# A projection as seven products of halves: the third pass of a two-layer attention block

## The chip, the cores and the metric

The kernel runs on one core of a Trainium2 chip. Everything is float32. The metric is the device time of one launch in microseconds (us), taken as the median of several executions. The profile and the trace come from one further execution. In them PE is TensorE (PEld its weight loads), DVE is VectorE, ACT is ScalarE, POOL is GpSimd and SP is SyncE, whose queue issues the DMA transfers.

## The reference

The input is `x` of shape (8, 256, 64, 64): eight images of 256 channels. Two layers are computed one after the other.

```python
# layer 0: softmax attention over keys from a 4x4-strided convolution
xr  = layernorm_c(conv(x, w_sr, stride=4))
q   = w_q @ x;  k, v = split(w_kv @ xr)
x   = x + gamma_s * (w_out @ softmax(q k / sqrt(32)) v)
# layer 1: relu linear attention on two sets of q, k, v
qkv = w_qkv @ x
agg = grouped_1x1(depthwise_5x5(qkv))
for part in (qkv, agg):                      # 32 heads of 8 channels each
    q, k, v = relu(part.q), relu(part.k), part.v with a column of ones
    o   = q @ (k.T @ v);  att = o[:, :8] / (o[:, 8] + 1e-15)
p   = w_proj @ concat(att_qkv, att_agg)      # 256 x 512 times 512 x pixels
y   = x + batchnorm(p)                       # a scale inv and a shift per channel
```

The change is in the last two lines. `w_proj` has 256 rows and 512 columns. Its input, for every pixel, is 256 channels of attention on `qkv` (called `att` in the kernel's third pass) and 256 channels of attention on `agg` (called `agg` there).

## The kernel before, in words

**Three passes.** The first pass computes layer 0 and the `qkv` planes, and writes both to device memory. The second pass computes the convolution, the sums k.T v of both parts, and the whole attention of the `agg` part. It writes the latter to the scratch tensors `attd`, one of shape (256, 2, 4, 512) for each image. The second pass works in 64 units of 32 channels of one image. In `applied(u, par)` it turns a tile `tok` of (pixel, channel) to (channel, pixel) with one DVE transpose, once for each of two column parities `par`. `stored(u, par)` writes each parity to memory in a transfer of its own, of 256 KB.

**The third pass** computes the attention of the `qkv` part, the projection, the scale and shift, and the sum with `x`. It works in 64 steps: 8 images, 2 halves of the image, and 4 pixel classes `cls` (the row and column parity of a pixel inside a 2x2 cell, as the planes were written). A step covers 512 pixels, in four groups of 128 that are named `f`, and all 256 output channels. In a step:

- `loads(n)` issues the transfers: `raw` (the q planes), `xs` (the x values), and every fourth step `agg`, 2 MB for half an image. When the fourth class of a half is done, the result tile `y` of 2 MB is stored.
- `flat(n)` makes `q` from `raw` with a ReLU, in four ACT instructions, one for each 128 channels and column parity.
- `applied(n, i)` for i = 0, 1 multiplies `q` with the block-diagonal sums `kvm` (four matmuls of 144 columns into `n`). ACT adds an epsilon to the denominators (`den`), DVE takes their reciprocals and multiplies them in, which gives `tok`.
- `turned(n, i)` transposes `tok` on PE into `at` (four 128x128 transposes), and ACT copies it to `att`.
- `proj(n, oc)` for the two output halves `oc` accumulates four matmuls of 512 columns in one PSUM bank `p` (two from `att`, two from `agg`). Two ACT instructions apply scale and shift and put the two column parities in their places in `z`. Two DVE instructions add `xs` into `y`.

A float32 matmul runs on PE as two passes, each with a weight load of its own, so the counts of the profile are two for each matmul; a transpose is one pass.

**What sets the order.** The kernel is written in program order, and a scheduler orders each engine's instructions from it by priorities and expected durations. The order is then fixed: each engine works through its own list, and waits on semaphores where an operand or a buffer is not ready. Tiles come from pools with a fixed number of buffers, and a new tile waits until all readers of the old one in its place are done. In the third pass `turned` runs half a step behind `applied`, and `proj` one step behind. The PSUM pools `p`, `n` and `at` each hold two tiles; a tile of `p` is one bank.

Of the kernel before, what the change touches and what calls it, by code (L numbers as in the profile page):

```python
# [27 lines left out]
F32 = mybir.dt.float32  # L28
# [4 lines left out]
P = 128  # L33
C = 256
# [926 lines left out]
def second_pass(ctx: ExitStack, tc: tile.TileContext, a, planes, kd, vd, wtd, kvd, attd):  # L961
# [234 lines left out]
    def applied(u, par):  # L1196
        t, k, b = units[u]
        q, bd = qs[u], bds[u]
        pn = bank("ng", f"ng_{u}_{par}", 1, 1024).rearrange("p (h n) -> p h n", h=4)
        for h in range(4):  # L1200
            nc.tensor.matmul(pn[:, h, : P + 16], q[:, par, h], bd[:, h], start=True, stop=True)
        den = late.tile([P, 2, 4, 16], F32, tag="den", name=f"den_{u}_{par}")
        nc.scalar.activation(den[:, 0], pn[:, :, P : P + 16], AF.Identity, bias=eps)
        nc.vector.reciprocal(den[:, 1], den[:, 0])
        tok = late.tile([P, 16, D0], F32, tag="tok", name=f"tok_{u}_{par}")
        nc.vector.tensor_tensor(
            tok.rearrange("p f (h e) -> p h f e", e=D1),
            pn[:, :, :P].rearrange("p h (f e) -> p h f e", e=D1),
            den[:, 1].unsqueeze(3).to_broadcast([P, 4, 16, D1]),
            ALU.mult,  # L1210
        )
        att = two.tile([P, 512], F32, tag="att", name=f"att_{u}_{par}", bufs=4)
        nc.vector.transpose(att, tok.rearrange("p f e -> p (f e)"))
        done[u, par] = att


    def stored(u, par):
        t, k, b = units[u]
        c0 = P * t + D0 * k
        tc.keep_in_program_order(  # L1220
            nc.sync.dma_start(attd[b][c0 : c0 + D0, par].rearrange("c j n -> j c n"), done.pop((u, par)))
        )

    positive(0)
    paired(0, 1)
    for u in range(n_all + 3):
        p, q, r = u - 1, u - 2, u - 3
        now, was, conv, out = u < n_all, 0 <= p < n_all, 0 <= q < n_all, 0 <= r < n_all
        if 0 < u < n_all:
            summed_raw(u)  # L1230
        if u + 1 < n_all:
            load_tokens(u + 1)
        if 0 < p < n_all:
            load_cells(p, 0)
        if was:
            stored_raw(p)
        if r > 0:
            stored(r - 1, 0)
            stored(r - 1, 1)
        if was:  # L1240
            summed(p)
        if now:
            convolve(u, 1, 2)
        if out:
            applied(r, 0)
        if u + 1 < n_all:
            paired(u + 1, 1)
        if now:
            convolve(u, 1, 0)
            if u == 0:  # L1250
                summed_raw(u)
            ended_raw(u)
            convolve(u, 1, 1)
        if u + 2 < n_all:
            load_cells(u + 2, 1)
        if was:
            ended(p)
        if conv:
            paired(q, 0)
            convolve(q, 0, 2)  # L1260
        if out:
            applied(r, 1)
        if conv:
            convolve(q, 0, 0)

        if u + 1 < n_all:
            positive(u + 1)
        if was:
            spread(p)
        if conv:  # L1270
            convolve(q, 0, 1)
        if now and u + B < n_all:
            b = units[u][2]
            load_weights(u + B - b, 1 if b < 4 else 0, b % 4)
    stored(n_all - 1, 0)
    stored(n_all - 1, 1)

# [1 line left out]
def third_pass(ctx: ExitStack, tc: tile.TileContext, a, planes, x2d, kvd, attd, out):  # L1281
# [10 lines left out]
        for tag in ("p", "n", "at")  # L1292
    }


    steps = [(b, half, cls) for b in range(B) for half in range(2) for cls in range(4)]
    n_all = len(steps)
    kvms, aggs, raws, xss, flats, atts, ys = {}, {}, {}, {}, {}, {}, {}

    msk = data.tile([P, P], F32, tag="msk", name="msk", bufs=1)  # L1300
    nc.sync.dma_start(msk, a.mask)
# [21 lines left out]
    def loads(n):  # L1323
# [10 lines left out]
                ],  # L1334
            )
        raws[n] = raw
        xs = data.tile([P, 2, 4, P], F32, tag="xs", name=f"xs_{n}", bufs=4)
        for c in range(2):
            nc.sync.dma_start(
                xs[:, c],  # L1340
# [5 lines left out]
        if cls == 0:  # L1346

            g = data.tile([P, 2, 2, 1024], F32, tag="agg", name=f"agg_{n}")
            for t in range(2):
                nc.sync.dma_start(  # L1350
                    g[:, t], attd[b][t * P : (t + 1) * P, :, 2 * half : 2 * half + 2].rearrange("c q j n -> c q (j n)")
                )
            aggs[b, half] = g.rearrange("p t q (j f n) -> p t (q j) f n", j=2, f=16)


    def flat(n):
        b, half, cls = steps[n]
        q = flattened.tile([P, 2, 4, P], F32, tag="q", name=f"q_{n}")
        col = cls % 2
        src = raws.pop(n).rearrange("p t f (y x) -> p t f y x", x=NB + 1)  # L1360
        for t in range(2):
            for par in range(2):
                nc.scalar.activation(
                    q[:, t, :, par * 64 : par * 64 + 64].rearrange("p f (y x) -> p f y x", y=8),
                    src[:, t, :, :, col + par : col + par + NB - 1 : 2],
                    AF.Relu,
                )
        flats[n] = q

    loads(0)  # L1370
# [18 lines left out]
    nc.vector.tensor_sub(shift, vec[:, 3], shift)  # L1389


    def applied(n, i):
        b, half, cls = steps[n]
        q, kvm = flats[n], kvms[b]
# [13 lines left out]
        )  # L1408
        return tok

    def turned(n, i, tok):
        if i == 0:
            atts[n] = late.tile([P, 2, 4, P], F32, tag="att", name=f"att_{n}")
        pa = psums["at"].tile([P, 512], F32, tag="at", name=f"at_{n}_{i}").rearrange("p (j n) -> p j n", j=4)
        for j in range(4):
            nc.tensor.transpose(pa[:, j], tok[:, j], ident)
        nc.scalar.copy(  # L1417
            atts[n][:, :, 2 * i : 2 * i + 2].rearrange("p t f n -> p f t n"),
            pa.rearrange("p (f t) n -> p f t n", f=2),
        )  # L1420

    def proj(n, oc):
        b, half, cls = steps[n]
        if cls == 0 and oc == 0:
            ys[b, half] = results.tile([P, 2, HW // 2], F32, tag="y", name=f"y_{b}_{half}")
        y = ys[b, half]
        yv = y.rearrange("p c (y a i x b j) -> p c a b i j y x", y=8, a=2, i=2, x=NB, b=2, j=2)
        ps = psums["p"].tile([P, 512], F32, tag="p", name=f"p_{n}_{oc}")
        for j in range(4):
            if j < 2:  # L1430
                src = atts[n][:, j].rearrange("p f (q n) -> p f q n", q=4)
            else:
                src = aggs[b, half][:, j - 2, :, 4 * cls : 4 * cls + 4].rearrange("p q f n -> p f q n")
            nc.tensor.matmul(  # L1434
                ps.rearrange("p (f q n) -> p f q n", f=4, q=4),
                wproj[:, j, oc * P : (oc + 1) * P],
                src,
                start=(j == 0),
                stop=(j == 3),
            )  # L1440
        z = late.tile([P, 4, P], F32, tag="z", name=f"z_{n}_{oc}")
        for par in range(2):
            nc.scalar.activation(  # L1443
                z.rearrange("p f (y x) -> p f y x", x=NB)[:, :, :, par::2],
                ps.rearrange("p (f q y x) -> p f q y x", f=4, q=2, y=8)[:, :, par],
                AF.Identity,
                bias=shift[:, oc : oc + 1],
                scale=inv[:, oc : oc + 1],
            )
        xs = xss[n]  # L1450
        for i in range(2):
            nc.vector.tensor_add(  # L1452
                yv[:, oc, cls // 2, cls % 2, i],
                z[:, 2 * i : 2 * i + 2].rearrange("p f (y x) -> p f y x", x=NB),
                xs[:, oc, 2 * i : 2 * i + 2].rearrange("p f (y x) -> p f y x", x=NB),
            )
        if cls == 3:
            cols = slice(half * (HW // 2), (half + 1) * (HW // 2))
            ready.append((out[b].rearrange("(c p) n -> p c n", p=P)[:, oc, cols], y[:, oc]))

    flat(0)
    last, ready = None, []
    for n in range(n_all + 1):
        if n + 2 < n_all:
            loads(n + 2)

            for dst, src in ready:
                tc.keep_in_program_order(nc.sync.dma_start(dst, src))
            ready = []
        if n + 1 < n_all:  # L1470
            flat(n + 1)
        for i in range(2):
            tok = applied(n, i) if n < n_all else None
            if last is not None:
                turned(*last)
            last = (n, i, tok) if n < n_all else None
            if n > 0:
                proj(n - 1, i)
        if n > 0:
            xss.pop(n - 1), atts.pop(n - 1)  # L1480
    for dst, src in ready:
        nc.sync.dma_start(dst, src)

# [2 lines left out]
def kernel_body(ctx: ExitStack, tc: tile.TileContext, a, out):  # L1486
# [15 lines left out]
    vd = [scratch(f"v_{b}", [8, NB2 + 2, NB2 + 2, P]) for b in range(B)]  # L1502
    kvd = {(b, t): scratch(f"kv_{b}_{t}", [4, 4, D0, D0 + 1]) for b in range(B) for t in range(2)}

    attd = [scratch(f"att_{b}", [C, 2, 4, 16 * D0]) for b in range(B)]
    wtd = [scratch(f"wt_{j}", [P, 16, 6 * P]) for j in range(4)]

    first_pass(tc, a, fine, planes, x2d, kd, vd, wtd)
# [120 lines left out]
```

## Time and profile before

The median is 4034.7 us (three runs, 4033.01 to 4037.88). The profiled execution spans 4031.7 us, at a granted TensorE clock of 0.99.

| stage | from, to (us) | PE busy | DVE busy | ACT busy | POOL busy |
|---|---|---|---|---|---|
| end of the second pass | 3220 to 3358 | 100% | 63% | 28% | 39% |
| passage to the third | 3358 to 3396 | 72% | 37% | 35% | 0% |
| third pass, steady | 3396 to 4009 | 99% | 45% | 49% | 0% |
| its end | 4009 to 4031.7 | 52% | 24% | 23% | 0% |

The figures are the busy times of the stages in a view by stretches, divided by their lengths. In the steady stage PE works nearly without a gap, DVE and ACT for half of the time, and POOL not at all. The DMA engines are busy for 0.71 of it.

### The profile page before, as it was taken

Reading aid. Unit: us, or ns where it says so; the run is one execution under the profiler, and the core shown is the slowest. Engines: PE = TensorE matmul, PEld = TensorE weight load, DVE = VectorE, ACT = ScalarE, POOL = GpSimd, SP = SyncE. Lnnn points to the kernel's source line nnn. Section 1 sums busy time; section 2 is a strip of 40 time slices with the busy share of each in tenths; the row PEclk is TensorE's granted clock in tenths of the full one; section 3 lists DMA queues with packets and bytes.
Section 4 is the critical chain, followed back from the end, with each engine's and each line's share of the span. In section 5 each row is a group of like instructions: output and inputs, shape, how many; then the busy total and the mean of one; then the engine's idle time right before and its main releaser. Section 6 shows DMA issues by size and latency. Waiting matters only on the chain. (4 is left out here: it accounts for less than half of the span.)

```text
span 4031.7 us, 69469 instructions
## 1 busy us (share of the span) xinstructions
PE 3967.1 (98%) x27266; PEld 2322.3 (58%) x27266; DVE 1943.0 (48%) x2724; ACT 1666.0 (41%) x3505; POOL 1207.0 (30%) x1234
## 2 busy tenths in 40 slices
PE   8999999999999999999999999999999998999998
PEld 4433433434334344343337888888888886565565
DVE  2554344343443434434444566666666664444443
ACT  2345455454554544545552222222222223454454
POOL 2333233332333333323333344444444440000000
PEclk9999999999999999999999999999999999999999
DMA  7655435344444344443539888778778756767674
GB/s 236 205 178 155 128 92 146 103 105 144 104 136 115 95 143 105 132 115 92 145 102 253 240 227 236 219 220 237 218 220 237 202 168 172 234 197 235 199 231 138
DMA packets 588321, 691.32 MB, mean 171 GB/s; under 512 B 62160, under 2 KB 431312, under 8 KB 583760
## 3 DMA queue, kind: packets, MB, share of 16 engines
q1 hardware_dynamic: 587984, 686.79, 59.7%
q8 instruction: 216, 3.54, 0.4%
q14 instruction: 121, 0.99, 0.1%
HBM read 412.54 MB, written 274.10 MB: 170 GB/s over the span
## 5 line engine op out<-in xcount | busy, mean ns | idle before, releaser
L786 POOL TENSOR_TENSOR e<-e,e 128x512 f32<-128x512 f32 x512 | 651.9, 1307 | 1204.1 <-PE av L775 1190.2
L799 DVE RECIPROCAL rden<-den 128x512 f32<-128x512 f32 x128 | 429.7, 3357 | 688.0 <-PE den L791 688.0
L764 ACT ACTIVATE e<-sc 128x512 f32<-128x512 f32 x1024 | 529.3, 602 | 419.2 <-PE sc L758 419.2
L834 PE MATMUL qkv<-x,wqkv 128*128 128x512 f32 x1536 | 701.1, 599 | 0.0
L834 PEld LDWEIGHTS qkv<-x,wqkv 128*128 128x128 f32 x1536 | 285.3, 190 | 372.7 <-issue 354.0
L1085 PE MATMUL cv<-w,c 128*128 128x128 f32 x3072 | 386.9, 280 | 4.9 <-POOL c L1029 4.9
L1085 PEld LDWEIGHTS cv<-w,c 128*128 128x128 f32 x3072 | 360.9, 193 | 33.5 <-issue 27.0
L853 DVE STREAM_TRANSPOSE turned<-qkv 128x512 f32<-128x512 f32 x256 | 177.3, 707 | 338.8 <-ACT stage L843 282.0
L758 PE MATMUL sc<-q,kk 32*128 32x512 f32 x2048 | 324.2, 640 | 11.0 <-DVE x L810 7.3
L1127 PE MATMUL sums<-vq,r 128*32 128x288 f32 x4096 | 303.1, 410 | 0.0
L1452 DVE TENSOR_TENSOR y<-z,xs 128x256 f32<-128x256 f32 x256 | 142.6, 644 | 315.9 <-ACT z L1443 290.9
L1101 ACT ACTIVATE r<-s 128x512 f32<-128x512 f32 x256 | 160.5, 627 | 299.9 <-DVE s L1100 299.5
L843 ACT COPY stage<-qkv 128x512 f32<-128x512 f32 x256 | 150.1, 586 | 304.3 <-PE qkv L834 294.6
L775 PE MATMUL av<-e,vv 128*32 128x512 f32 x2048 | 274.3, 608 | 0.0
L1443 ACT ACTIVATE z<-p,bn 128x256 f32<-128x256 f32 x256 | 133.7, 578 | 314.5 <-PE p L1434 240.6
L1089 PE MATMUL cv<-c,w 128*128 128x128 f32 x2048 | 256.4, 279 | 0.0
L743 PE MATMUL q<-x,wq 128*128 128x512 f32 x512 | 253.8, 618 | 0.0
L1434 PE MATMUL p<-att,wproj 128*128 128x512 f32 x512 | 249.4, 609 | 2.2 <-ACT att L1417 2.2
L1092 ACT COPY both<-cv 128x512 f32<-128x512 f32 x128 | 75.0, 586 | 421.8 <-PE cv L1085 364.8
L1434 PE MATMUL p<-agg,wproj 128*128 128x512 f32 x512 | 242.3, 596 | 0.0
L1089 PEld LDWEIGHTS cv<-c,w 128*128 128x128 f32 x2048 | 242.2, 194 | 0.0
L671 PE MATMUL sr<-x,wsr 128*128 128x256 f32 x1024 | 234.6, 385 | 7.1 <-DMA wsr<-in_w_sr_dram 7.1
(121 smaller groups left out, 5107.8 us busy)
## 6 DMA issues: line engine op xcount, KB each, us to landing
vq<-v SPq DMA_DIRECT2D x256, 384.0 KB
planes<-stage SPq DMA_DIRECT2D x256, 289.0 KB
d<-planes SPq DMA_DIRECT2D x128, 578.0 KB
raw<-planes SPq DMA_DIRECT2D x128, 272.0 KB
x<-in_xp_dram SPq DMA_DIRECT2D x64, 512.0 KB
wsr<-in_w_sr_dram SPq DMA_DIRECT2D x128, 256.0 KB
x<-x SPq DMA_DIRECT2D x128, 256.0 KB
k<-turned SPq DMA_DIRECT2D x256, 128.0 KB
```

Source lines behind the costliest of these rows:

```text
L671: nc.tensor.matmul(ps[:, oc], w[:, ci, oc * P : (oc + 1) * P], xt[:, ci, f * NK : (f + 1) * NK], start=(f == ci == oc == 0), stop=(f == R ...
L743: nc.tensor.matmul(ps, consts["wq"][:, ci, c * P : (c + 1) * P], x_tiles[b][:, ci, s * QB : (s + 1) * QB], start=(ci == 0), stop=(ci == 1),)
L758: nc.tensor.matmul(scs[h], kks[b][rows, c, kc * P : (kc + 1) * P], qs[rows], start=True, stop=True)
L764: nc.scalar.activation(e, scs[h], AF.Exp, scale=D0**-0.5)
L775: nc.tensor.matmul(sums["av"][cols], vvs[b][:, kc, c * P + h * D0 : c * P + (h + 1) * D0], es[h], start=(kc == 0), stop=(kc == 1),)
L786: nc.gpsimd.tensor_tensor(es0[h], es0[h], es1[h], ALU.add)
L799: nc.vector.reciprocal(r, den)
L834: nc.tensor.matmul(ps, consts["wqkv"][:, ci, j * P : (j + 1) * P], x_tiles[b][:, ci, s * QB : (s + 1) * QB], start=(ci == 0), stop=(ci == 1),)
L1085: nc.tensor.matmul(out, x, m, start=(da == 0), stop=(da == 1))
L1089: nc.tensor.matmul(out, m, x, start=(da == 0), stop=(da == 1))
L1127: nc.tensor.matmul(ps[h * D0 : (h + 1) * D0, : 36 * D1].rearrange("p (r n e) -> p r n e", r=3, e=D1), kt[:, par, h, 2 * r + c], vq[:, r : ...
L1434: nc.tensor.matmul(ps.rearrange("p (f q n) -> p f q n", f=4, q=4), wproj[:, j, oc * P : (oc + 1) * P], src, start=(j == 0), stop=(j == 3),)
```

## The change

The projection of a step is a product of a 256 x 512 matrix and a 512 x 512 matrix of pixels. It is cut into a 2 x 2 scheme: the rows of `w_proj` into two output halves `oc`, its columns into the `agg` and the `att` half, and the pixels into two halves i = 0, 1. Done directly these are eight products of quarters. The change uses the scheme of Strassen, in Winograd's form, which needs seven. Each product is a 128 x 256 by 256 x 256 product: two matmuls of 256 columns, four passes. The weights of the seven are the quarters `a11`, `a12`, `a21`, `a22` and their combinations `s1` to `s4` and `minus`, formed once at the start of the pass, with the scale `inv` multiplied in. The right sides are `agg` and `att` of either half and four combinations `t1` to `t4`, formed in every step: `t1` on DVE (`early_side`), the other three on POOL (`late_sides`).

The four quarters of the result share partial sums. The change keeps three regions in PSUM: `x` and `y` side by side in one bank, `z` in another. Four products go to `x` one after the other, and each adds to what is there. After each, ACT or DVE reads the sum so far before the next product comes on top of it.

Around this, three things follow. The `agg` output of the second pass is stored with the column parities interleaved, in one transfer of 512 KB for each unit, so that `flat` needs two ACT instructions instead of four, and the results need no reordering by parity. The loop of the third pass is one step longer, since the products run two steps behind `applied`. Half of the additions of `xs` move from DVE to POOL.

```diff
-        att = two.tile([P, 512], F32, tag="att", name=f"att_{u}_{par}", bufs=4)
-        nc.vector.transpose(att, tok.rearrange("p f e -> p (f e)"))
+        if par == 0:
+            done[u] = two.tile([P, 16, D0, 2], F32, tag="att", name=f"att_{u}")
+        nc.vector.transpose(done[u][:, :, :, par], tok)
...
         for t in range(2):
-            for par in range(2):
-                nc.scalar.activation(... 128x256 ..., AF.Relu)
+            nc.scalar.activation(
+                q[:, t].rearrange("p f (y x) -> p f y x", y=8), src[:, t, :, :, col : col + NB], AF.Relu
+            )
...
+    nc.vector.tensor_mul(wproj, wproj, wide.unsqueeze(1).to_broadcast([P, 4, C]))
+    a11, a12, a21, a22 = (wproj[:, k : k + 2, oc * P : (oc + 1) * P] for oc in range(2) for k in (2, 0))
+    nc.vector.tensor_add(s1, a21, a22)
+    nc.vector.tensor_sub(s2, s1, a11)
+    nc.vector.tensor_sub(s3, a11, a21)
+    nc.vector.tensor_sub(s4, a12, s2)
+    nc.scalar.mul(minus, a22, -1.0)
...
+    def early_side(n):
+        nc.vector.tensor_sub(sides[n][:, 0], agg(n, 1), agg(n, 0))
+    def late_sides(n):
+        nc.gpsimd.tensor_tensor(t2, raw1, t1, ALU.subtract)
+        nc.gpsimd.tensor_tensor(t3, raw1, agg(n, 1), ALU.subtract)
+        nc.gpsimd.tensor_tensor(t4, t2, raw0, ALU.subtract)
...
+    def first_products(n):
+        xy, zb = (psums["p"].tile([P, 512], F32, tag=f"p{i}", name=f"p{i}_{n}", bufs=1) for i in range(2))
+        product(n, x, a11, agg(n, 0), first=True)
+        nc.scalar.activation(parts[n][:, 0], x, AF.Identity, bias=shift[:, 0:1])
+        product(n, y, a12, atts[n][:, 0].rearrange("p t (j n) -> p t j n", j=2))
+        nc.vector.tensor_add(quarter(n, 0, 0), split(parts[n][:, 0]), split(y))
+    def second_products(n):
+        product(n, x, s2, sides[n][:, 1])
+        nc.scalar.activation(parts[n][:, 1], x, AF.Identity, bias=shift[:, 0:1])
+        product(n, z, s1, sides[n][:, 0], first=True)
+        nc.scalar.activation(parts[n][:, 2], z, AF.Identity, bias=shift[:, 1:2])
+    def third_products(n):
+        product(n, x, s3, sides[n][:, 2])
+        nc.vector.tensor_add(quarter(n, 1, 1), split(parts[n][:, 2]), split(x))
+    def fourth_products(n):
+        product(n, x, minus, sides[n][:, 3])
+        nc.scalar.activation(quarter(n, 1, 0), split(x), AF.Identity, bias=shift[:, 1:2])
+        product(n, z, s4, atts.pop(n)[:, 1].rearrange("p t (j n) -> p t j n", j=2))
+        nc.vector.tensor_add(quarter(n, 0, 1), split(parts.pop(n)[:, 1]), split(z))
...
+        (nc.vector if i else nc.gpsimd).tensor_tensor(
+            yv[:, oc, cls // 2, cls % 2, i], outs[n][:, oc, i]..., xss[n][:, oc, 2 * i : 2 * i + 2]..., ALU.add,
+        )
...
-    for n in range(n_all + 1):
+    for n in range(n_all + 2):
+        m = n - 2
+        first_products(m); flat(n + 1); applied(n, 0); early_side(n)
+        finished(m, 0, 0); second_products(m); turned(n - 1, 1); late_sides(n - 1)
+        third_products(m); applied(n, 1); turned(n, 0)
+        finished(m, 1, 1); fourth_products(m); finished(m, 1, 0); finished(m, 0, 1)
```

The loop at the end is given as the order of its calls; the conditions for the first and last steps are left out.

## The prediction

> **What bounds the kernel now.** I first read the busy shares over the span, where PE has 98%, and then the third pass alone, since the change works only there and in two small places before it. The groups of instructions from 3400 to 4000 us show what a step of it is made of: columns are the count, the busy time, the mean ns of one, and the idle time before it with its releaser.
>
> ```profile
> L1434 PE MATMUL p<-att,wproj 128*128 128x512 f32 x481 | 232.5, 606 | 0.0
> ...
> L1398 PE MATMUL n<-kvm,q 128*128 128x144 f32 x962 | 147.6, 286 | 0.0
> ...
> L1452 DVE TENSOR_TENSOR y<-z,xs 128x256 f32<-128x256 f32 x240 | 133.8, 645 | 292.5 <-ACT z L1443 267.5 <-DMA agg<-att 10.5 <-DMA xs<-x 7.0
> ...
> L1363 ACT ACTIVATE q<-raw 128x256 f32<-128x256 f32 x240 | 89.6, 465 | 0.0
> ...
> L1417 ACT COPY att<-at 128x512 f32<-128x512 f32 x120 | 70.8, 590 | 8.0 <-PE at L1416 3.8
> ```
>
> Its PE groups have no idle time; ACT and DVE wait for each other and for PE. So PE's list sets the time. A PE duration contains the drain of the pipeline; the pace is read from starts. The timeline of PE in one step (start, duration, what, passes):
>
> ```profile
> 3612.47 0.41 PE L1398 MATMUL n<-kvm,q 128*128 128x144 f32 x2
> 3612.71 0.60 PE L1416 MATMUL at<-ident,tok 128*128 128x128 f32 x4
> 3613.15 1.88 PE L1434 MATMUL p<-att,wproj 128*128 128x512 f32 x4
> 3614.87 1.88 PE L1434 MATMUL p<-agg,wproj 128*128 128x512 f32 x4
> 3616.58 1.14 PE L1398 MATMUL n<-kvm,q 128*128 128x144 f32 x8
> 3617.56 0.60 PE L1416 MATMUL at<-ident,tok 128*128 128x128 f32 x4
> 3618.00 0.90 PE L1398 MATMUL n<-kvm,q 128*128 128x144 f32 x6
> 3618.84 1.98 PE L1434 MATMUL p<-att,wproj 128*128 128x512 f32 x4
> 3620.66 1.88 PE L1434 MATMUL p<-agg,wproj 128*128 128x512 f32 x4
> 3622.38 0.41 PE L1398 MATMUL n<-kvm,q 128*128 128x144 f32 x2
> ```
>
> A step is 3622.38 - 3612.47 = 9.91 us. Starts give 0.4285 us for a pass of 512 columns (1.715 for four), 0.1225 for 144 columns (0.98 for eight), 0.11 for a transpose. Sixteen, sixteen and eight of them are 6.86 + 1.96 + 0.88 = 9.70. The other 0.21 lies at 3618.84, the one product that has to wait (for ACT's copy of `att`): six passes that need 0.735 take 0.84, and the four behind them take 1.82 instead of 1.715. So a wait that PE meets costs the wait itself plus about 0.11 for a weight load that is no longer hidden.
>
> **What the Trainium skill says.** "TensorE: Matmul & The Clock Gate", section "Architectural detail: the array is 16x 32x32, not 1x 128x128", says that PE's queue can pull weight loads ahead of running matmuls. The trace agrees: passes of 144 columns follow each other every 0.12 us although a load lasts 0.19. "PSUM — Partial Sum Buffer", section "PSUM bank collisions raise a hardware error", says that two engines must not be in one bank at the same time, even at other columns, and that semaphores should guard whole banks. In the changed kernel's list PE indeed waits for DVE's read of `y` before it writes `x` in the same bank. No such pair is in the third pass before. "SBUF — State Buffer", section "Who interferes with whom", says that a DVE instruction with two SBUF inputs and a GpSimd instruction that reads SBUF exclude each other for the whole instruction. The second pass shows it:
>
> ```profile
> 2663.49 1.28 POOL L1061 TENSOR_TENSOR red_raw<-kq 128x512 f32<-128x512 f32 x1 [1.19 <-ACT kq L1068]
> 2663.86 1.49 DVE L1025 TENSOR_TENSOR c<-d 128x544 f32<-128x544 f32 x1 [0.65 <-DMA d<-planes]
> ...
> 2664.85 1.09 POOL L1062 TENSOR_TENSOR red_raw<-red_raw 128x256 f32<-128x256 f32 x1
> 2665.28 1.25 DVE L1026 TENSOR_TENSOR c<-d 128x544 f32<-128x544 f32 x1
> ```
>
> The DVE operation takes 0.72 elsewhere; here it ends 0.58 after POOL's end, and POOL's next ends 0.59 after DVE's.
>
> **PE's work after.** Seven products of four passes are 28 passes of 256 columns. The first pass has such a shape: sixteen of `sr` take from 680.65 to 684.10, so 0.2155 each, loads hidden. That is 6.03 us instead of 6.86. The other passes stay: 6.03 + 1.96 + 0.88 = 8.87.
>
> **The waits that come with it.** PE's order in a step of the changed kernel is: `n0` (2 passes), x1 (`agg` by `a11`), `n0` (6), y, z, three transposes, x2 (`s2`), one transpose, `n1` (4), x3 (`s3`), `n1` (4), four transposes, x4 (`minus`), z again (`s4`). Every x waits for a reader of the bank. From the trace: PE's last issue to ACT's start 0.25 (3612.47 to 3612.72), ACT's end to PE 0.05. ACT reading 256 columns: a copy takes 0.37 (L726), and a bias pointer adds 0.1 (64 columns with bias 0.31, 36 without 0.19), so 0.47. DVE on 256 columns from PSUM: 0.42 (L687). Laid out from 0:
>
> - x1 ends at 1.11. ACT has read it, and y may start, at 1.11 + 0.25 + 0.47 + 0.05 = 1.88; `n0` fills until 1.84. Wait 0.04, load 0.11.
> - y ends at 2.85, z at 3.71, transposes at 4.04. DVE gets to y only behind the reciprocal (0.53) and `tok` (0.69) of `n0`: 2.45 to 3.77; then 0.42 less 0.10 overlap, at PE by 4.14. Wait 0.10, load 0.11: x2 ends at 5.11.
> - x3 needs ACT's read of x2: 5.88, against 5.71 filled. Wait 0.17, load 0.11: ends at 6.85.
> - x4 needs DVE's read of x3 at 7.57; `n1` and transposes fill until 7.78. No wait. It ends at 8.64, z at 9.50.
> - The next x1 needs ACT's read of x4. In ACT's list this stands behind `den` of `n1`, two `flat` and an `att` copy, started at 7.34 + 0.25 and spaced 0.19, 0.50, 0.47, 0.50 (an operation's 0.115 overlap with the next as in the trace; a `flat` of 512 elements as L1101, 0.62). It ends at 9.72, so PE may go at 9.77, against 9.75.
>
> This gives 9.50 without the last wait and 9.63 with it and its load. If the weight load is hidden even behind a wait, the same walk gives 9.33. I take 9.50.
>
> **ACT, DVE, POOL.** ACT sheds two `flat`, and has four reads of 0.47 for four `z` of 0.58. DVE sheds two y additions, and gets `t1` (0.69 as L800, 512 elements from SBUF twice) and three reads: 2x0.53 + 2x0.69 + 3x0.42 + 2x0.64 + 0.69 = 5.7 us in a step. POOL gets three of 512 elements (1.27, the unhindered L1061) and two y additions of 256 (0.73 as L1062; with strided output up to 0.9, no row): 5.3 to 5.6. `t2` to `t4` have nearly a step until PE needs them. Three DVE operations (two y, `t1`) can each be held for up to 1.13 by POOL; in my layout two are, y behind `t2` and the last y behind `t4`, and DVE still reaches the next reciprocal in time.
>
> **Edits at nothing.** The second pass's transposes write every other element: at most tens of ns each in a DVE that idles 37% there, behind a PE at 100%. The larger `att` and `agg` transfers move the same bytes; DMA is at 0.71 and would go to 0.74. The weight combinations (some 3.5 us of DVE) fall in the passage, where PE waits for `raw` until 3388.
>
> **Ends.** Before, from the last `n` (4009.2) PE needs 12.9 us, the last y 2.4, the store 7.2: 22.5. After, a rest of 2.2 and two steps of products without fill remain (6.0 and its waits each): about 17.8 for PE, 1.3 for y, and both output halves end together, so 3.5 more for the store (1 MB at some 300 GB/s): 29.8. But the last `n` stands 2.5 earlier in its step. That makes 5 worse. At the start two steps carry no products, which may gain 4 in the passage. I book 1 in all. Between the ends stand 61 steps: 61 x (9.91 - 9.50) = 25. So 4034.7 - 25 + 1 = 4010.7, say 4010.
>
> **The rivals.**
> - *The waits stay hidden* (0.2): 9.05 a step (8.87 and one small wait), if reads are shorter than I think. For it: no wait exceeds 0.17 in the layout. Against: the order has no reserve at three of the six products. 61 x 0.86 - 1 = 51: 3984.
> - *The waits eat the gain* (0.1): four exposed loads and waits of 0.25 each, 9.85: 4032, no change.
> - *DVE and POOL become the bound* (0.2), slower: DVE's 5.7 with dependent gaps 5.9, and three holds of 1.13 make 9.3; if POOL's additions take 1.6 instead of 1.27, three of 1.46 make 10.3, and `tok` and the bank's reads come late: 61 x 0.35 = 21: 4056. For it: the exclusion above. Against: the unhindered durations of L1061 and L1062.
>
> **The numbers.** Forecast (0.5): 4010. The range 3984 to 4042 leaves out the tails of the first and last rival. Faster by over 0.2%: the forecast and the first rival, plus a little: 0.71. Same: 0.09. Slower: 0.2.
>
> **What would show it.** Right: PE's idle before x2, x3 and y, released by DVE and ACT, of 0.1 to 0.2; 28 passes spaced 0.2155; steps near 9.5. Wrong: steps under 9.2 or over 9.8; waits of PE on POOL's `sides`; `tok` held behind y or `t1`; or PE waiting for `raw` or `agg`.

## The result, and the profile after

The changed kernel takes 4055.5 us (median of five runs, 4053.83 to 4062.98); the kernel before, beside it, 4035.8 (4033.01 to 4037.88). The ratio is 1.0054, with a 95% interval of 1.0039 to 1.0069: slower, where 4010 was forecast. The profiled execution spans 4052.8 us at a granted clock of 0.99, 21.1 us more than before.

First, where these lie. ACT treats the denominators 128 times in the third pass, once for each `n`, so the starts of its `den` instructions in the timeline give a mark for every half step. Stage one ends at the mark of step 8, the second lasts 48 steps to the mark of step 56, the third is the rest.

| kernel | to step 8 | 48 steps | rest | a quiet step |
|---|---|---|---|---|
| before | 3459.2 | 475.8 | 96.7 | 9.91 |
| after | 3462.0 | 486.8 | 104.0 | 10.02 |
| difference | 2.8 | 11.0 | 7.3 | 0.11 |

A quiet step is one in which no sums of a new image are prepared. So the steps became longer, and not 0.4 shorter. The groups of the changed kernel between 3400 and 4000 us (columns as before) say who waits:

```profile
L1461 PE MATMUL p<-sides,combined 128*128 128x256 f32 x934 | 250.8, 391 | 29.4 <-DVE z L1486 25.1 <-DVE z L1498 0.6
...
L1417 PE MATMUL n<-kvm,q 128*128 128x144 f32 x936 | 153.8, 287 | 0.0
...
L1514 DVE TENSOR_TENSOR y<-z,xs 128x256 f32<-128x256 f32 x118 | 136.8, 1160 | 3.7
...
L1448 DVE TENSOR_TENSOR sides<-agg 128x512 f32<-128x512 f32 x59 | 65.4, 1109 | 0.0
```

PE, which had no idle time in its groups before, now waits 25.1 us for one DVE instruction: L1486, the read of `y` out of the bank that `x` is in. And two DVE groups last nearly twice as long as they should: the addition of `xs` 1160 ns on average for the same 128x256 elements that took 645 before, and `t1` (L1448) 1109 where 690 was taken. The timeline of PE over one step of the changed kernel, from one x2 to the next (start, duration, what, passes):

```profile
3598.17 1.10 PE L1461 MATMUL p<-sides,combined 128*128 128x256 f32 x4 [0.30 <-DVE z L1486]
3599.11 0.27 PE L1437 MATMUL at<-ident,tok 128*128 128x128 f32 x1
3599.22 0.66 PE L1417 MATMUL n<-kvm,q 128*128 128x144 f32 x4
3599.93 1.10 PE L1461 MATMUL p<-sides,combined 128*128 128x256 f32 x4
3600.87 0.65 PE L1417 MATMUL n<-kvm,q 128*128 128x144 f32 x4
...
3603.52 0.41 PE L1417 MATMUL n<-kvm,q 128*128 128x144 f32 x2
3603.88 1.13 PE L1461 MATMUL p<-agg,wproj 128*128 128x256 f32 x4
3604.84 0.90 PE L1417 MATMUL n<-kvm,q 128*128 128x144 f32 x6
3605.58 1.12 PE L1461 MATMUL p<-att,wproj 128*128 128x256 f32 x4
3606.54 1.03 PE L1461 MATMUL p<-sides,combined 128*128 128x256 f32 x4
3607.40 0.49 PE L1437 MATMUL at<-ident,tok 128*128 128x128 f32 x3
3608.18 1.10 PE L1461 MATMUL p<-sides,combined 128*128 128x256 f32 x4 [0.29 <-DVE z L1486]
```

Starts again give the pace. A product whose loads are hidden takes 0.86 to the next start (3606.54 to 3607.40), as forecast. Against that: x1 (L1461 from `agg`) starts 0.11 late and takes 0.10 more, y (from `att`) takes 0.10 more, x2 starts 0.45 late (three transposes need 0.33 after 3607.40) and takes 0.08 more, x3 (3599.93) starts 0.22 late and takes 0.08 more. Together 1.14, and 8.87 + 1.14 = 10.01.

Now DVE in the same step, which is what x2 waits for:

```profile
3601.14 0.42 DVE L1498 TENSOR_TENSOR z<-parts,p 128x256 f32<-128x256 f32 x1 [3.11 <-PE p L1461]
3601.59 1.73 DVE L1514 TENSOR_TENSOR y<-z,xs 128x256 f32<-128x256 f32 x1
3603.16 0.52 DVE L1420 RECIPROCAL den<-den 128x64 f32<-128x64 f32 x1
3603.79 0.69 DVE L1422 TENSOR_TENSOR tok<-n,den 128x512 f32<-128x512 f32 x1
3604.40 1.16 DVE L1448 TENSOR_TENSOR sides<-agg 128x512 f32<-128x512 f32 x1
3605.48 0.41 DVE L1505 TENSOR_TENSOR z<-parts,p 128x256 f32<-128x256 f32 x1
3605.93 0.62 DVE L1514 TENSOR_TENSOR y<-z,xs 128x256 f32<-128x256 f32 x1
3606.38 0.53 DVE L1420 RECIPROCAL den<-den 128x64 f32<-128x64 f32 x1
3607.02 0.69 DVE L1422 TENSOR_TENSOR tok<-n,den 128x512 f32<-128x512 f32 x1
3607.63 0.41 DVE L1486 TENSOR_TENSOR z<-parts,p 128x256 f32<-128x256 f32 x1
```

From 3601.14 to 3608.04 DVE has no pause: ten instructions, 6.90 us. Before it, DVE stood idle 3.11 us for x3. So the step is a loop over three engines: x2 0.94, to ACT 0.20, ACT's read 0.47, to PE 0.15, x3 0.94, to DVE 0.27, these ten instructions 6.90, to PE 0.15, and x2 again: 10.02. DVE is busy for about two thirds of the step and sets its length all the same, since its idle time all lies where it waits for x3. The line that is long is the addition at 3601.59. POOL at that time:

```profile
3600.34 1.27 POOL L1453 TENSOR_TENSOR sides<-att,sides 128x512 f32<-128x512 f32 x1 [1.50 <-ACT att L1438]
3601.56 1.27 POOL L1454 TENSOR_TENSOR sides<-att,agg 128x512 f32<-128x512 f32 x1
3602.79 1.53 POOL L1455 TENSOR_TENSOR sides<-sides,att 128x512 f32<-128x512 f32 x1
3604.28 0.73 POOL L1514 TENSOR_TENSOR y<-z,xs 128x256 f32<-128x256 f32 x1
```

The addition started just as `t2` ended (3601.61), and 0.03 after the start of `t3`, which went ahead of it: the addition ends at 3603.32, 0.49 after `t3`'s end. `t1` at 3604.40 was held by POOL's own addition (to 3605.01).

### The profile page after: what moved, and what is told of

Read it like the earlier page. It is cut to its first block, busy times and chain, and to the rows that moved or that the text cites. A ratio compares the mean times of both kernels' runs of the same rounds, so it can differ in the third digit from the quotient of the medians.

```text
span 4052.8 us, 71866 instructions
## 1 busy us (share of the span) xinstructions
PE 3950.9 (97%) x28038; PEld 2470.1 (61%) x28038; DVE 2088.9 (52%) x2860; ACT 1632.7 (40%) x3379; POOL 1553.9 (38%) x1554
## 4 chain that ended last, share of the span: by engine, by line
PE 88%; DMA 4%; DVE 4%; issue 2%; POOL 1%; SPq 1%; ACT 0%; DVEq 0%; POOLq 0%; ACTq 0%
PE qkv L834 16%; PE p L1461 9%; PE cv L1085 8%; PE cv L1089 8%; PE sc L758 7%; PE sums L1127 7%; PE av L775 6%; PE q L743 6%; PE sr L671 5%; PE o L809 5%; PE ng L1201 3%; PE den L791 3%; PE n L1417 3%; DMA wt<-wb 1%; PE raw L1110 1%
## 5 line engine op out<-in xcount | busy, mean ns | idle before, releaser
L1461 PE MATMUL p<-sides,combined 128*128 128x256 f32 x1024 | 275.1, 392 | 33.3 <-DVE z L1486 26.4
L671 PEld LDWEIGHTS sr<-x,wsr 128*128 128x128 f32 x1024 | 194.2, 191 | 63.8 <-issue 37.1
L809 PE MATMUL o<-att,wout 128*128 128x512 f32 x512 | 230.8, 593 | 0.0
L758 PEld LDWEIGHTS sc<-q,kk 32*128 32x128 f32 x2048 | 97.3, 183 | 216.8 <-issue 118.3
```

The source lines that it names most:

```text
L671: nc.tensor.matmul(ps[:, oc], w[:, ci, oc * P : (oc + 1) * P], xt[:, ci, f * NK : (f + 1) * NK], start=(f == ci == oc == 0), stop=(f == R ...
L758: nc.tensor.matmul(scs[h], kks[b][rows, c, kc * P : (kc + 1) * P], qs[rows], start=True, stop=True)
L809: nc.tensor.matmul(ps, consts["wout"][:, c, oc * P : (oc + 1) * P], att[c], start=(c == 0), stop=(c == 1))
L1461: nc.tensor.matmul(place.rearrange("p (j n) -> p j n", j=2), w[:, t], x[:, t], start=first and t == 0, stop=t == 1, skip_group_check=True,)
```

## The experiments

Theory: PE's work fell as forecast, and the steps are long because x2, in the bank that `y` shares, waits for a read that stands last in DVE's run, with POOL's holds ahead of it. Rivals: the holds on DVE are the cause by themselves (POOL as the bound), the order of PE's list is the cause, or the new layout of `attd`, with what goes with it, costs time.

**A bank for y.** The pool `at` gives up one of its banks for it.

```diff
-        xy, zb = (psums["p"].tile([P, 512], F32, tag=f"p{i}", ...) for i in range(2))
-        banks[n] = x, y, z = xy[:, :C], xy[:, C:], zb[:, :C]
+        xb, yb, zb = (psums["p"].tile([P, 512], F32, tag=f"p{i}", ...) for i in range(3))
+        banks[n] = x, y, z = xb[:, :C], yb[:, :C], zb[:, :C]
...
-        product(n, y, a12, atts[n][:, 0]...)
+        product(n, y, a12, atts[n][:, 0]..., first=True)
```

> y gets a bank of its own (the transposes' pool gives up its second one), so PE no longer waits for DVE's read of y before x2, and the scheduler puts y's passes between the x products. Theory 1 (a loop x3, DVE's read of x3, the y addition held by POOL, reciprocals, tok, t1, the read of y, x2, ACT, x3 sets the step at 10.02 us): the loop is cut, the step falls to 9.0 to 9.3, the time to 3995 to 4010. Theory 2 (DVE or POOL have too much work in a step, whatever the bank): the step stays at 9.8 or more, the time above 4035. Theory 3 (PE pays for many small waits and exposed weight loads, whoever causes them): 9.6 to 9.8, 4025 to 4040.

3986.8 us, ratio 0.9879 (0.9862 to 0.9895): 1.2% faster than before. The timeline of PE, from one x4 to the next:

```profile
3605.18 1.03 PE L1461 MATMUL p<-sides,combined 128*128 128x256 f32 x4
...
3614.07 1.03 PE L1461 MATMUL p<-sides,combined 128*128 128x256 f32 x4
```

8.89 us, PE's work alone, and below the 9.0 to 9.3 that was expected. But DVE is held here too, as its own line and POOL's show:

```profile
3613.38 1.04 DVE L1514 TENSOR_TENSOR y<-z,xs 128x256 f32<-128x256 f32 x1
```

```profile
3612.65 1.28 POOL L1453 TENSOR_TENSOR sides<-att,sides 128x512 f32<-128x512 f32 x1 [0.61 <-ACT att L1438]
3613.89 1.53 POOL L1454 TENSOR_TENSOR sides<-att,agg 128x512 f32<-128x512 f32 x1
```

Nobody on PE waits for it. The run does not separate two things, since with a bank more the scheduler also put PE's list in another order, with `n` or transposes or another product ahead of each use of `x`.

**All additions of xs on POOL**, which takes DVE's first hold away, and **t2 to t4 as constants**, which takes POOL's three long operations away:

```diff
-        (nc.vector if i else nc.gpsimd).tensor_tensor(
+        nc.gpsimd.tensor_tensor(
```

> All four additions of xs go to POOL; the bank is still shared. Theory 1: DVE's stretch from the read of x3 to the read of y loses 1.73 and some 0.5 of its 6.9 us, and no longer bounds; what is left are the waits of the layout, 9.5 to 9.6 a step, 4020 to 4030. Theory 2 in the form that POOL is the bound: POOL's work grows from 5.3 to 6.8 us, the step grows with it, over 4060. Theory 3: 9.8 or more, 4045 to 4055.

```diff
-        nc.gpsimd.tensor_tensor(t2, raw1, t1, ALU.subtract)
-        nc.gpsimd.tensor_tensor(t3, raw1, agg(n, 1), ALU.subtract)
-        nc.gpsimd.tensor_tensor(t4, t2, raw0, ALU.subtract)
...
-        product(n, x, s2, sides[n][:, 1])
+        product(n, x, s2, fixed[:, 0])
```

> t2, t3 and t4 are not computed: the products read a constant tile in their place (left out: three of POOL's five operations in a step). Nothing of DVE's own list changes. Theory 1: DVE's y addition behind x3 falls from 1.73 to 0.64 us and t1 towards 0.69, so the loop shrinks by over 1 us and no longer bounds: 9.4 to 9.6 a step, 4015 to 4030. Theory 3: the holds are beside the point, 4045 or more. DVE alone too long: 4045 or more as well.

4048.4 us (ratio 1.0038, 1.0024 to 1.0053) with quiet steps of 9.84, and 4029.8 (0.9986, 0.9977 to 0.9995) with steps of 9.71. Neither step is as short as the theory had it (9.5 to 9.6, and 9.4 to 9.6), and the first run is what had been written for many small waits. So the holds are worth 0.2 to 0.3 of a step and not more. (In the second run `t1` also came out behind the read of `y` in DVE's list, so its figure is not that of the holds alone.) In the first, DVE waits for ACT's `den` ahead of both reciprocals, hence has time to spare, and x2 is still 0.28 late, since the three transposes ahead of it need only 0.33:

```profile
3606.53 0.55 DVE L1420 RECIPROCAL den<-den 128x64 f32<-128x64 f32 x1 [1.22 <-ACT den L1419]
```

```profile
3607.75 0.49 PE L1437 MATMUL at<-ident,tok 128*128 128x128 f32 x3
3608.36 1.10 PE L1461 MATMUL p<-sides,combined 128*128 128x256 f32 x4
```

The chain from the end of `n` over `den`, reciprocal, `tok` and the read of `y` takes longer than what PE has to do until x2. The holds make a wait longer that is there without them. ACT's `den` ends 0.03 before the reciprocal here and 0.22 before it in the changed kernel, and this 0.19 is what the step gained.

**The layout alone**: the eight products of before, with the new `attd`, two `flat` for four, and one ACT instruction of 512 for two of 256 in each output half.

```diff
-        for par in range(2):
-            nc.scalar.activation(z...[:, :, :, par::2], ps...[:, :, par], AF.Identity, bias=..., scale=...)
+        nc.scalar.activation(z.rearrange("p f n -> p (f n)"), ps, AF.Identity, bias=..., scale=...)
```

> The eight products of before, with agg stored in the order of blocks, two ReLU instructions instead of four, one evacuation of 512 columns instead of two. PE has the list of before: 9.9 us a step. If the 14 us that the changed kernel loses outside the steady steps come from the stores or the order of loads: 4042 to 4050. If they come from the products' start and end: 4030 to 4037, no change.

4037.8 us, ratio 1.0010 (1.0001 to 1.0019). Its quiet steps are 9.91 as before, its 48 steps 475.7; it is at step 8 at 3465.7 in place of 3459.2, and its rest is 1.1 shorter. By the medians this part costs some 3 us, and not in the steps. In the two traces the loss lies ahead of step 8, but 2.4 of its 6.5 us are there already at the eighth `den` from the end of the second pass (3334.02 against 3331.61), before the passage begins.

**The program's order in the shared bank.** In the program the order is x1, y, `n`, x2, z, transposes, x3, `n`, transposes, x4, z. Each PE instruction of the third pass is pinned behind the one before it:

```diff
-            nc.tensor.matmul(
-                place..., w[:, t], x[:, t], start=first and t == 0, stop=t == 1, skip_group_check=True,
-            )
+            tc.keep_in_program_order(
+                nc.tensor.matmul(
+                    place..., w[:, t], x[:, t], start=first and t == 0, stop=t == 1, skip_group_check=True,
+                )
+            )
```

> The bank stays shared by x and y as in the changed kernel; only TensorE's matrix products of the third pass are pinned in the order of the program: x1, y, n of the first half, x2, z, transposes, x3, n of the second half, transposes, x4, z2. If the order is the cause (each product on the bank follows too soon on the last reader of it, and the quarter that x2 waits for stands behind reciprocal and tok in VectorE's list): other work lies ahead of x2, x3 and x4, steps of 8.9 to 9.1 us, 3985 to 4000 us. If the sharing of the bank itself is the cause (x2 waits for VectorE's reader of y in any order, and VectorE is held by GpSimd): steps of 9.6 us or more, 4025 to 4050 us.

4070.6 us, ratio 1.0090 (1.0073 to 1.0107), a quiet step 10.17: the slowest of all, and beyond what either expectation named. The timeline of PE:

```profile
3610.79 1.03 PE L1466 MATMUL p<-att,combined 128*128 128x256 f32 x4
3612.01 1.13 PE L1466 MATMUL p<-agg,wproj 128*128 128x256 f32 x4 [0.19 <-ACT z L1509]
3613.70 1.13 PE L1466 MATMUL p<-att,wproj 128*128 128x256 f32 x4 [0.56 <-ACT parts L1490]
```

x2, x3 and x4 no longer wait, as the order theory had it. But y, behind x1 in the same bank, now waits for ACT's read of x1: x1 would be done at 3612.98, y starts at 3613.70. In this order it is another pair of the shared bank that stands too close. x1 too waits 0.36, for ACT's read of x4.

**The changed kernel's order with a bank for y.** PE's list is pinned as it is in the changed kernel, and DVE's came out in the changed kernel's order too, so that only the banks differ:

```diff
         product(n, x, a11, agg(n, 0), first=True)
         nc.scalar.activation(parts[n][:, 0], x, AF.Identity, bias=shift[:, 0:1])
+        yield
-        product(n, y, a12, ...)
+        product(n, y, a12, ..., first=True)
...
+        next(n0, 0)
+        next(n0, 0)
+        next(first, 0)
+        list(n0)
...
+        list(first)
```

> y has a bank of its own, and TensorE's list is pinned in the order that the changed kernel has (n, x1, n, y, z, transposes, x2, n, x3, n, transposes, x4, z2). If the sharing of the bank is the cause: x2 waits for nobody on VectorE, steps of 9.1 us or less, 3990 to 4003 us. If the order is the cause: the waits of x1, y and x3 stay (about 0.6 us of the 0.97), steps of 9.4 to 9.6 us, 4015 to 4035 us.

4016.2 us, ratio 0.9953 (0.9937 to 0.9970), a quiet step 9.38. DVE's addition is held for 1.75 here, as in the changed kernel, and x2 comes on time:

```profile
3612.78 0.49 PE L1444 MATMUL at<-ident,tok 128*128 128x128 f32 x3
3613.11 1.03 PE L1473 MATMUL p<-sides,combined 128*128 128x256 f32 x4
3613.98 0.27 PE L1444 MATMUL at<-ident,tok 128*128 128x128 f32 x1
```

So with order and holds as they are, sharing costs 10.02 - 9.38 = 0.64 of a step (x2's 0.45 and 0.08, and y's 0.10). The step is still about what had been written for the order as the cause: the remaining 0.5 over PE's 8.87 are the waits for ACT at x1 and x3 with their loads, and the order of the first experiment, in which PE waits for nobody, takes these away. Of the 1.13 that the first experiment gave back, 0.64 are thus the bank's, and 0.49 the order's once the bank is there.

**The read of y earlier on DVE.** The bank is shared, PE's list pinned as it was, and on DVE the read of `y` stands ahead of the reciprocal and `tok` of the next `n`:

```diff
-        nc.vector.reciprocal(den[:, 1], den[:, 0])
+        rec = nc.vector.reciprocal(den[:, 1], den[:, 0])
+        if n > 1 and i == 0:
+            tc.keep_in_program_order(rec)
```

> x and y share the bank as in the changed kernel, and TensorE's list is pinned as there; on VectorE alone the read of y (the first quarter) is pinned ahead of the reciprocal and tok of the next n instead of behind them. If the place of the reader in VectorE's list, with what holds VectorE ahead of it, makes x2's wait: x2 no longer waits, only y's weight load (0.10) and the waits of x1 and x3 stay, steps of 9.4 to 9.55 us, 4015 to 4030 us. If the sharing costs whatever the place of the reader (as in the run in program order): steps of 9.8 us or more, 4040 us or more.

4027.6 us, ratio 0.9977 (0.9970 to 0.9984), a quiet step 9.49. DVE in that step:

```profile
3613.39 0.62 DVE L1533 TENSOR_TENSOR y<-z,xs 128x256 f32<-128x256 f32 x1
3614.28 0.42 DVE L1504 TENSOR_TENSOR z<-parts,p 128x256 f32<-128x256 f32 x1 [0.27 <-PE p L1477]
3614.62 0.55 DVE L1428 RECIPROCAL den<-den 128x64 f32<-128x64 f32 x1
```

DVE now waits for PE's y, not PE for DVE, and x2 follows its transposes after 0.33 without a wait:

```profile
3614.84 0.49 PE L1448 MATMUL at<-ident,tok 128*128 128x128 f32 x3
3615.17 1.03 PE L1477 MATMUL p<-sides,combined 128*128 128x256 f32 x4
```

One exchange in DVE's list, with nothing less to do on any engine and POOL's hold still 1.75, gives back 0.53 of a step.

**Both**, the bank and all additions on POOL:

> y in its own bank and all four additions of x on GpSimd. If with the bank of its own TensorE's work is the only bound: the same 8.9 us a step and 3980 to 3990 us, whether VectorE is held at y or not. If the holds still cost something there: below 3980 us. If GpSimd (5.6 us a step, now 1.0 more) holds others up: above 3995 us.

3988.8 us, ratio 0.9884 (0.9868 to 0.9901), 8.89 a step: as with the bank alone. Once PE does not wait for DVE's run, its holds cost nothing in a quiet step, and POOL, with all four additions, does not bound it.

**The sums of the next image.** In the first kernel with a bank for y, steps 8 to 12 take 11.05 and steps 16 to 20 take 10.06 where the others take 8.89, and DVE waits 13.2 us for `kvp`, the sums of a new image; behind it in DVE's list is all that PE needs. (The kernel before waits for `kvp` too, but 8.8 of its 9.3 us fall ahead of step 8, so it is no comparison for these steps.) First the transfers were issued earlier:

```diff
+        if n == 0:
+            fetch_sums(0)
+            fetch_sums(1)
         if cls == 0 and half == 0:
             load_sums(b)
+        if cls == 0 and half == 1 and b + 2 < B:
+            fetch_sums(b + 2)
```

> y in its own bank, and the transfers of the sums kvp of image b + 2 issued half an image after the start of image b (those of images 0 and 1 at the start) instead of just ahead of use. With the bank alone, steps 8 to 12 and 16 to 20 take 11.05 and 10.05 us where the others take 8.9, and VectorE waits 13.2 us for kvp. If VectorE, held in order at that transfer, is the cause: these steps fall to 8.9 to 9.1 us, 11 to 13 us less, 3973 to 3978 us. If the transfers of that stretch (raw, agg, x) are late themselves: those steps stay above 9.8 us, 3983 to 3990 us.

> The changed kernel with the same early transfers of kvp and nothing else. If VectorE held at kvp costs it too: steps 8 to 12 fall from 10.7 to about 10.1 us, 3 to 4 us less than the changed kernel, 4050 to 4053 us. If the transfers of that stretch are late themselves: no less, 4054 to 4058 us.

3986.4 us (0.9878, 0.9863 to 0.9893) with the bank, and 4056.3 (1.0053, 1.0039 to 1.0066) without it. Neither moved, and the view of waits says why; for the bank with early transfers it has

```profile
DVE kvp L1312 <- DMA kvp<-kv: 13.2, 4, 4.1
```

(us in total, times, longest): the same wait. The scheduler had taken later images' transfers and their first sums forward together (with the bank, the first sum of the last image ran at 3538.5 and its second at 3680.0), so these runs did not test the theory. Pinning both in the program's order did:

```diff
+            d = nc.sync.dma_start(kvps[b][:, t], kvd[b, t].rearrange("f k d n -> (k d) f n"))
+            if b > 1:
+                tc.keep_in_program_order(d)
...
+        s = nc.vector.tensor_add(kvp[:, :, :2], kvp[:, :, :2], kvp[:, :, 2:])
+        if b > 0:
+            tc.keep_in_program_order(s)
```

> y in its own bank; the transfers of kvp half an image ahead as in the last two runs, and now pinned in the order of the program on the transfer queue, as is the first sum of kvp on VectorE, so that neither is taken forward past earlier work (in the last two runs both were, and VectorE waited for kvp as long as before). If VectorE, held in order at kvp, makes the long steps 8 to 12 and 16 to 20: no wait for kvp, these steps at 8.9 to 9.2 us, 3973 to 3978 us. If other late transfers make them: they stay above 9.8 us, 3983 to 3990 us.

> The changed kernel with kvp transferred ahead and pinned in the same way, and nothing else. If VectorE held at kvp costs the changed kernel too: steps 8 to 12 fall from 10.7 to about 10.1 us, 3 to 5 us less than the changed kernel, 4050 to 4053 us. If not: 4054 to 4058 us.

With the bank: 3974.5 us, ratio 0.9855 (0.9839 to 0.9870). All groups of four steps from step 8 on take 8.89 to 8.92, and the 48 steps 427.0 in place of 440.6. This is the best version found, 1.5% faster than before. Without the bank: 4055.7 (1.0053, 1.0039 to 1.0067), no less than the changed kernel. There the wait for `kvp` is gone and steps 8 to 12 fall from 10.70 to 10.02, as was expected, but each group of four steps in which an image's sums are formed takes 10.36 a step in place of 10.1 to 10.2. The six DVE instructions for it stand in one piece in the loop here, and cost 4 x 0.34 = 1.4 us an image; spread over the step as in the changed kernel they cost 0.5 to 0.9.

## Why the prediction was wrong

- *PE's work, 9.70 to 8.87*: right. With the waits away a step is 8.89.
- *The layout of the waits, 9.50*: the places were right, and this is the step that failed. A quiet step is 0.52 longer than laid out. Of this, 0.32 lie in the term for x2, "Wait 0.10, load 0.11", which measured 0.45 and 0.08, and 0.21 at x1, whose wait had been seen as possible and left out. The others fit: y 0.10 (0.15 forecast), x3 0.30 (0.28).
- *Why x2's term was too small*: the layout let the reciprocal of `n0` start as soon as ACT had `den`, since "DVE still reaches the next reciprocal in time". It does not: it comes 0.22 after `den` instead of 0.05. The holds themselves were not larger than the bound of 1.13: the addition behind x3 was held for 1.11, `t1` for 0.47, and the last y not at all. What had not been added up is DVE's run. In the layout it begins 0.25 after x3, at 7.10, and the reciprocal of the next step stands at 9.50 + 2.45 = 11.95, so 4.85 later. The seven DVE operations between come to 4.03 by the prediction's own durations, and to 6.29 with its two holds, which is too long even with 0.1 of overlap at each of the seven. The trace has 5.24. The rest of x2's excess is the wake from DVE to PE (0.15 in the changed kernel, not 0.05) and the wait of 0.04 ahead of y that did not come, so that PE stood ready sooner. These and x1's wait are there as well in the run at 9.84, where DVE has time to spare, so 9.50 would have been missed without the holds too. That a bank's wait is small when its reader does not stand behind other work was tested: with the read of `y` moved, the step is 9.49.
- *Two sums*: "2.45 to 3.77" is 0.10 more than 0.53 and 0.69. The trace has such a gap (0.11 between reciprocal and `tok`), but the text does not name it. The same walk with all loads hidden comes to about 9.3, where 9.33 is written. Neither changes the outcome.
- *POOL at 5.3 to 5.6 us*: right (1.27, 1.27, 1.53 and twice 0.73 make 5.5), and PE in quiet steps never waits for its sides. The third rival came nearest in kind: DVE, held by POOL, does close the loop, and "the bank's reads come late". But it needed POOL operations of 1.6 us and a held `tok`, where `t2` and `t3` keep their 1.27 and `tok` its 0.69, and with the first hold away the step is still 9.84. That its time, 4056, is the measured one is luck: it came from 61 steps of 0.35 more each, and a quiet step is 0.11 longer.
- *Edits at nothing*: by the medians the layout alone costs some 3 us (the interval allows 0.4 to 8), ahead of step 8; which of its edits does it was not tried.
- *Ends*: the tail from the last `n` was forecast 29.8 and is about 29. But the 4 us gained in the passage, and the 2.5 from an earlier last `n`, do not show: the changed kernel is 2.8 later at step 8. The work for each new image was not in the sum: it was hidden in a DVE with time to spare, and in the loop it is not. The 48 steps lose 11.0, of which 0.11 x 48 = 5 are what every step loses, and the rest lies in the steps with `kvp`.

Two places of the Trainium skill have a number here. "PSUM — Partial Sum Buffer", section "PSUM bank collisions raise a hardware error", says to guard by bank and not by address. The lists do, and these runs give the price of that in this order: 0.64 us in a step of 10.02. "SBUF — State Buffer", section "Who interferes with whom", says that issue order decides who is blocked, for a whole instruction. The trace agrees: the addition that started 0.03 after `t3` was held for 1.11, nearly all of `t3`'s 1.27.

## What to carry to other kernels

When products share a bank, list for each one the last reader of the bank, the engine that it is on, and all that stands ahead of it in that engine's list: what counts is when that run ends, not how long the reader takes. Then add up such a loop around all engines, holds included, before trusting a share of busy time, since an engine that is busy for two thirds may set the step. And work that was hidden in an engine with time to spare (here an image's sums and the wait for their transfer) has to be priced again when the change puts this engine in the loop.

## What the runs showed of the hardware that was not expected

- Where one POOL operation hands over to the next, 0.03 us decide what a DVE addition with both inputs in SBUF pays. In the changed kernel it started 0.03 after `t3`, and 0.02 before the end of `t2`: it took 1.73 in place of 0.62, and `t3` its usual 1.27. In the kernel with a bank for y it started 0.51 ahead of `t3`: it took 1.04, went in between the two, and `t3` took 1.53.
- A product that has a wait ahead of it takes 0.08 to 0.11 more than its 0.86, and y does so although its start is not late (0.96 in the changed kernel; 0.86 with a bank of its own in the same order). In the changed kernel y's first weight load starts 0.01 ahead of the product, at 3605.57, and that of the product behind it 0.22 ahead, at 3606.32. Four such products in a step made 0.36 of the 1.14 us.
